# The end of an RNN-and-attention kernel rewritten as one written list: who subtracts the maxima, where transposes go, when outputs are projected

## The chip, the cores and the metric

The kernel runs on one core of a Trainium2 chip, in fp32 throughout. The metric is the time of one execution in microseconds (us) on the device; the figure of a kernel is the median of several executions. A profile is one further execution, recorded by the hardware profiler.

## The reference, cut to what matters

The input `x` has shape (2, 2048, 256). Layer one is a recurrent layer on the normalized input with a residual; layer two is an attention layer whose values and outputs are mixtures of five experts, again on the normalized input with a residual. Only the second layer and its end bear on this case:

```python
e, d, dh = Wv.shape                       # 5, 256, 64; 8 heads
wv = _topk_mask(gl_v, SEL) * sigmoid(gl_v)
xv = einsum('btd,edk->btek', x, Wv)
v = einsum('bthe,btek->bhtk', wv, xv)
scores = einsum('bhid,bhjd->bhij', q * scale, k)
probs = softmax(scores, axis=-1)
attn = einsum('bhij,bhjd->bihd', probs, v)
mask_o = _topk_mask(gl_o, SEL)
out = einsum('bthe,bthk,ekd->btd', mask_o, attn, Wo)
```

So each (batch, head) has 2048 x 2048 scores, a softmax over the keys, a product with the values; each head's result is then spread over the five experts that its mask selects (320 numbers per position), summed over the heads, and multiplied by `Wo` as one 320 x 256 product. The result is added to the residual and written out.

## The kernel before, in words

The recurrent layer takes the first 120 us or so and is left alone by the change. After it, `x1d` in DRAM holds the residual stream.

**Units, steps and tiles.** The attention is cut into 64 units (`units`): 16 (batch, head) pairs by four blocks of 512 queries. A unit has eight tiles of scores; a tile is two blocks of 128 keys by 512 queries, 128 x 1024 numbers, and its index is `t` (unit 63 has tiles 504 to 511, unit 62 has 496 to 503). One step `T` of the loop at the end of the function makes two tiles, so a unit takes four steps (`U_T`), and there are 256 steps (`NT`).

**What happens to a tile.** `scores` (L634) multiplies on TensorE into a PSUM tile of two banks (pool `ps_s`, two buffers, four banks). `stage` (L645) copies it to SBUF on ScalarE; `largest` (L655 to L661) keeps the running maximum on VectorE. When a unit's eight tiles are in, `turn_max` and `reduce_max` (L668, L673) turn the maxima with four TensorE transposes and reduce them on VectorE, and `spread_max` (L683, L686) transposes the result back so that all partitions hold each query's maximum, once in PSUM (`pt`) and, copied by ScalarE, once in SBUF (`top`). `subtract` (L693) takes the maximum off a staged tile: tiles 0 and 1 of a unit on VectorE from `pt`, the others on GpSimd from `top`; in the last unit tiles 0, 1, 2, 4 and 6 are VectorE's. `exponential` (L696) is ScalarE's. `products` (L706) accumulates P.V on TensorE into `o`. `fold` (L718) adds a tile's odd partner into it by a DMA that accumulates, issued from GpSimd, so that `sums` (L727), which accumulates the softmax's denominators on TensorE, takes half as many tiles; in the last unit nothing is folded and all eight tiles are summed. A tile's second half of life runs `LAG` = 6 steps behind its scores.

**The end of a unit.** `take` (L742, L743) and `take_sums` (L749, L750) bring `o` and the sums `d` to SBUF; `weigh` (L759 to L768) transposes them and works out reciprocal times mask; `close` (L772) makes the 320 wide product `pro` on VectorE; `gather` (L814, L817) adds `pro` into `yd` in DRAM, or, for the last head, into `y` in SBUF that `fetch_y` (L793) has brought, on GpSimd. `close_last` (L772, L804) does the same for the very last unit on VectorE, 128 positions at a time.

**The outputs.** 16 blocks of 128 positions per batch. `turn_out` transposes a block of `y` (`py`, L829, three transposes), copies it to one of two `yT` tiles on ScalarE (L833, L836), and loads the residual `z` from `x1d` (L838, on SP's queue). `project_out` multiplies by `Wo` (`pz`, L846, twelve matmuls that the profile counts as 24), adds `pz` into `z` on VectorE (L854), and stores `z` (L855, SP). `z` has two buffers (pool `ap`, `bufs=2`), so the load of block c+2 waits until the store of block c has landed. The small PSUM tiles `pm`, `pt`, `po`, `py`, `pz` all come from `misc`, two banks in turn.

**What sets the order.** Each engine executes its queue in order. The order is written by hand: three tables (`before`, `first_behind`, `behind`) say which helper is called in which step, and the loop over `T` runs over `NT + LAG + 1` steps, so that the last seven steps do only what lags behind. The outputs of the last two units (blocks 8 to 15 of batch 1) and the `close_last` between them are queued in one piece in the last step. There is no planner; within this part the compiler keeps the traced order on each engine, and it places tiles in the banks that their pools come to hold.

Of the kernel before, what the change touches and what calls it, by code (L numbers as in the profile page):

```python
# [8 lines left out]
F32 = mybir.dt.float32  # L9
# [5 lines left out]
P = 128  # L15
# [5 lines left out]
def rnn_then_switchhead_kernel(  # L21
# [15 lines left out]
    nc = tc.nc  # L37
# [82 lines left out]
    def misc(shape, nm):  # L120
        return ps_m.tile(shape, F32, tag="m", name=nm)
# [95 lines left out]
    def choose(pool, b, c0, n, half, nm, logits):  # L217
# [16 lines left out]
        for d in range(1, E):  # L234
            a = pool.tile([P, n, H, E - d], F32, tag=f"later{d}", bufs=1 + (d > 1), name=f"lt{nm}_{d}")
            nc.vector.tensor_tensor(a, g0[:, :, :, d:E], g[:, :, :, 0 : E - d], ALU.is_gt)
            later.append(a)
# [324 lines left out]
    four = ctx.enter_context(tc.tile_pool(name="four", bufs=1))  # L562
    ps_s = ctx.enter_context(tc.tile_pool(name="ps_s", bufs=2, space=PSUM))
    ps_o = ctx.enter_context(tc.tile_pool(name="ps_o", bufs=1, space=PSUM))
    units = [(i, n) for i in range(len(heads)) for n in range(NQ)]
    NT = len(units) * U_T
# [81 lines left out]
    def largest(t, ss):  # L648
# [13 lines left out]
        m_of.pop(u)  # L662

    def turn_max(u):
        pm = misc([P, QS, P], f"pm{u}")
        mm = mm_of.pop(u)
        for s in range(QS):
            nc.tensor.transpose(pm[:, s, :], mm[:, s * P : (s + 1) * P], ident)  # L668
        mx_of[u] = (pm, ap.tile([P, QS], F32, tag="mq", name=f"mq{u}"))
# [5 lines left out]
    def spread_max(u):  # L675
        _, mq = mx_of.pop(u)
        if u == len(units) - 1:
            pt = ps_s.tile([P, 2, QB], F32, tag="s", name=f"pt{u}")[:, 0, :]
            pt = pt.rearrange("p (s q) -> p s q", q=P)
        else:  # L680
            pt = misc([P, QS, P], f"pt{u}")
        for s in range(QS):
            nc.tensor.transpose(pt[:, s, :], mq[:, s : s + 1].to_broadcast([P, P]), ident)  # L683
        pt = pt.rearrange("p s q -> p (s q)")
        top_of[u] = (pt, ap.tile([P, QB], F32, tag="top", name=f"top{u}"))
        nc.scalar.copy(top_of[u][1], pt)  # L686

    def subtract(t):
        u, c = t // HC, t % HC
        p = ring[t]  # L690
        last = u == len(units) - 1 and c % 2 == 0
        eng, top = (nc.vector, top_of[u][0]) if c < 2 or last else (nc.gpsimd, top_of[u][1])
        eng.tensor_tensor(p, p, top.unsqueeze(1).to_broadcast([P, 2, QB]), ALU.subtract)  # L693
# [100 lines left out]

    def close_last(u):

        i, n = units[u]
        b, _ = heads[i]
        po, mr = weigh(u)
        y = y_of[b, n]  # L800
        pr = four.tile([P, QS, E, DH], F32, tag="pro", bufs=1, name=f"pro{u}")
        for s in range(QS):
            masked(pr[:, s : s + 1], po, mr, s, 1)
            nc.vector.tensor_tensor(y[:, s], y[:, s], pr[:, s], ALU.add)  # L804

    def gather(u):
# [18 lines left out]
    def turn_out(b, c):  # L825
        yf = y_of[b, c // QS][:, c % QS].rearrange("p e k -> p (e k)")
        py = misc([P, len(o_chunks), P], f"py{b}_{c}")
        for k, (r0, m) in enumerate(o_chunks):
            nc.tensor.transpose(py[0:m, k, :], yf[:, r0 : r0 + m], ident)  # L829
        yT = yT_all[yT_of["n"] % 2]  # L830
        yT_of["n"] += 1
        full = sum(m == P for _, m in o_chunks)
        nc.scalar.copy(yT[:, 0:full, :], py[:, 0:full, :])  # L833
        for k, (r0, m) in enumerate(o_chunks):
            if m < P:
                nc.scalar.copy(yT[0:m, k, :], py[0:m, k, :])  # L836
        z = ap.tile([P, D], F32, tag="z", name=f"z{b}_{c}")
        nc.sync.dma_start(out=z, in_=x1d[c, :, b, :])  # L838
        yT_of[b, c] = (yT, z)
# [137 lines left out]
    for u, (i, n) in enumerate(units):  # L977
        b, h = heads[i]
        T1 = (u + 1) * U_T
        at(first_behind, T1, spread_max, u)  # L980
        outs = [(b, n * QS + s) for s in range(QS)]
        if u == len(units) - 1:

            outs = [(b, c) for c in range(n * QS - QS, n * QS + QS)]
            todo = [(turn_out, *outs[0])]
            for k, o in enumerate(outs):
                todo += [(turn_out, *x) for x in outs[k + 1 : k + 2]] + [(project_out, *o)]
            at(behind, T1 + LAG - 1, fetch_y, u)
            for x in todo[:3] + [(take_sums, u), (close_last, u)] + todo[3:]:
                at(behind, T1 + LAG, *x)  # L990
            continue
        at(behind, T1 + LAG + 1, take_sums, u)
        at(behind, T1 + LAG + 2, close, u)
        at(behind, T1 + LAG + 3, gather, u)
        if h == H - 1:
            at(behind, T1 + LAG, fetch_y, u)
            if u < len(units) - 2:
                T = T1 + LAG + 4
                for o, t, p in zip(outs, (0, 1, 3, 3), (1, 2, 3, 4)):
                    at(before if o[1] % QS == 2 else behind, T + t, turn_out, *o)  # L1000
                    at(behind if o[1] % QS == 2 else before, T + p, project_out, *o)

    with tc.manual_schedule():
        for T in range(NT + LAG + 1):
            new = (2 * T, 2 * T + 1) if T < NT else ()
            sub = [t for t in (2 * (T - LAG + 1), 2 * (T - LAG + 1) + 1) if 0 <= t < 2 * NT]
# [9 lines left out]
            ss = [scores(t) for t in new]  # L1016
            if new:
                stage(new[0], ss[0])
            if T % U_T == 0:
                if new:  # L1020
                    stage(new[1], ss[1])
                if 0 < T <= NT:
                    turn_max(T // U_T - 1)
                    reduce_max(T // U_T - 1)
                if new:
                    largest(new[1], ss[1])
            elif new:
                largest(new[1], ss[1])
                stage(new[1], ss[1])
            if fresh:  # L1030
                subtract(sub[0])
            if T % U_T and new:
                largest(new[0], ss[0])
# [4 lines left out]
            k = T - LAG  # L1038
            if 0 < k < NT - U_T + 1:
                fold(2 * (k - 1))  # L1040
# [4 lines left out]
            for t in old:  # L1045
                products(t)
            if 3 <= k and k % 2 and k - 3 < NT - U_T:
                t = 2 * (k - 3)
                sums(t, t + 2, t % HC == 0, t % HC != 0)
            if NT - 2 <= k < NT:  # L1050

                t0 = 2 * (NT - U_T)
                for t in range(t0, t0 + 4, 2) if k == NT - 2 else ():
                    sums(t, t + 1, t == t0, False)
                sums(2 * k, 2 * k + 1, False, k == NT - 1)
            if sub:
                exponential(sub[0])
            for f in first_behind.pop(T, []) + behind.pop(T, []):
                f()
        assert not before and not behind and not first_behind  # L1060


# [44 lines left out]
```

## Time and profile before

| | |
|---|---|
| median of 3 runs | 1616.0 us (1615.15 to 1617.99) |
| the profiled execution's own time | 1618.95 us |
| its span, first to last instruction | 1617.2 us |
| mean granted TensorE clock | 0.992 |
| busy: TensorE, VectorE, ScalarE, GpSimd | 95%, 80%, 77%, 79% of the span |
| end of the last scores | about 1546.4 us |
| first and last add of an output of batch 1 (L854) | 1549.7 and 1613.8 us |

The page of the profile gives busy time by engine, then the span in 40 slices; views can be asked for any stretch of it. In a view by windows each row is a stretch with its length, then busy time and number of instructions of each engine, then the granted clock and the DMA's share. In a list of groups, a row has the line, engine, operation, output<-inputs, shapes and count, then busy time and mean ns of one, then the idle time just ahead. The profile counts an fp32 matmul as two or more instructions.

### The profile page before, as it was taken

Reading aid. Unit: us, or ns where it says so; the run is one execution under the profiler, and the core shown is the slowest. Engines: PE = TensorE matmul, PEld = TensorE weight load, DVE = VectorE, ACT = ScalarE, POOL = GpSimd, SP = SyncE. Lnnn points to the kernel's source line nnn. Section 1 sums busy time; section 2 is a strip of 40 time slices with the busy share of each in tenths; the row PEclk is TensorE's granted clock in tenths of the full one; section 3 lists DMA queues with packets and bytes.
Section 4 is the critical chain, followed back from the end, with each engine's and each line's share of the span. In section 5 each row is a group of like instructions: output and inputs, shape, how many; then the busy total and the mean of one; then the engine's idle time right before and its main releaser. Section 6 shows DMA issues by size and latency. Waiting matters only on the chain.

```text
span 1617.2 us, 29233 instructions
## 1 busy us (share of the span) xinstructions
PE 1540.3 (95%) x11442; PEld 593.7 (37%) x11442; DVE 1297.6 (80%) x1808; ACT 1251.0 (77%) x1617; POOL 1285.5 (79%) x856
## 2 busy tenths in 40 slices
PE   6989899999999999999999999999999999999996
PEld 5984233333333333333334333333333333333233
DVE  7472889998988888888987769898889888888762
ACT  4664688888878888888887778888888888888861
POOL 3053699888888988999997868898889898889870
PEclk9998999999999999999999999999999999999998
DMA  5021368788888888787886767788888888888752
GB/s 162 1 106 31 105 152 192 163 187 179 173 167 173 173 172 174 157 178 164 171 188 156 168 143 187 154 177 171 174 165 176 176 169 170 169 170 170 165 130 83
DMA packets 86623, 252.26 MB, mean 156 GB/s; under 512 B 11920, under 2 KB 31184, under 8 KB 86480
## 3 DMA queue, kind: packets, MB, share of 16 engines
q0 software_dynamic: 43200, 163.60, 54.0%
q1 hardware_dynamic: 41648, 86.13, 17.5%
q8 instruction: 91, 1.49, 0.4%
q10 hardware_dynamic: 1632, 0.61, 0.1%
q14 instruction: 52, 0.43, 0.1%
HBM read 59.46 MB, written 50.33 MB: 68 GB/s over the span
## 4 chain that ended last, share of the span: by engine, by line
PE 67%; DVE 12%; DMA 6%; ACT 3%; issue 2%; POOL 2%; SPq 0%; DVEq 0%; ACTq 0%; POOLq 0%
PE s L634 23%; PE o L706 20%; PE d L727 6%; DVE m L655 5%; DMA p<-p 4%; PE pk L140 4%; PE pq L159 3%; PE pz L846 2%; ACT p L645 2%; PE pt L683 2%; DVE pro L772 2%; PE pm L668 1%; POOL p L693 1%; PE po L759 1%; DVE p L693 1%
## 5 line engine op out<-in xcount | busy, mean ns | idle before, releaser
L693 POOL TENSOR_TENSOR p<-p,top 128x1024 f32<-128x1024 f32 x381 | 1057.2, 3027 | 11.8 <-ACT top L686 11.7
L645 ACT COPY p<-s 128x1024 f32<-128x1024 f32 x512 | 511.0, 1011 | 152.8 <-DVE m L655 66.9
L696 ACT ACTIVATE p<-p 128x1024 f32<-128x1024 f32 x512 | 538.0, 1062 | 49.5 <-DVE p L693 37.1
L634 PE MATMUL s<-qs,k 64*128 64x512 f32 x1024 | 511.8, 617 | 6.4 <-ACT p L645 6.3
L634 PE MATMUL s<-q,k 64*128 64x512 f32 x1024 | 511.8, 617 | 4.0 <-ACT p L645 3.2
L706 PE MATMUL o<-p,v 128*32 128x512 f32 x4096 | 491.5, 597 | 10.2 <-DVE os L743 7.7
L655 DVE TENSOR_TENSOR m<-s,m 128x1024 f32<-128x1024 f32 x320 | 390.9, 1222 | 96.4 <-PE s L634 87.7
L718 POOL DMA_DIRECT2D p<-p x252 | 341.4, 1355 | 60.0 <-PE o L706 21.5
L706 PEld LDWEIGHTS o<-p,v 128*32 128x32 f32 x4096 | 113.5, 109 | 297.8 <-issue 156.4
L634 PEld LDWEIGHTS s<-qs,k 64*128 64x128 f32 x1024 | 169.1, 186 | 144.1 <-ACT p L645 47.9
L634 PEld LDWEIGHTS s<-q,k 64*128 64x128 f32 x1024 | 169.1, 185 | 138.7 <-issue 52.4
L693 DVE TENSOR_TENSOR p<-p,pt 128x1024 f32<-128x1024 f32 x131 | 158.5, 1210 | 0.1
L727 PE MATMUL d<-p,ones 128*32 128x512 f32 x1040 | 153.1, 593 | 5.1 <-DMA p<-p 5.0
L655 DVE TENSOR_TENSOR m<-s,p 128x1024 f32<-128x1024 f32 x64 | 78.4, 1225 | 57.5 <-ACT p L645 57.1
L814 POOL DMA_DIRECT2D yd<-pro x48 | 45.2, 942 | 92.0 <-DVE pro L772 89.8
L772 DVE TENSOR_TENSOR pro<-po,mr 128x1280 f32<-128x1280 f32 (+1 forms) x67 | 95.9, 1431 | 2.7
L619 DVE TENSOR_TENSOR xq<-xq,wp 128x1280 f32<-128x1280 f32 x60 | 89.2, 1487 | 2.3 <-DVE wp L617 0.2
L625 DVE TENSOR_REDUCE v<-xq 128x256 f32<-128x1280 f32 x60 | 88.6, 1477 | 0.0
L727 PEld LDWEIGHTS d<-p,ones 128*32 128x32 f32 x1040 | 37.5, 110 | 97.2 <-issue 76.8
L159 PE MATMUL pq<-xn2T,wq 128*32 128x512 f32 x512 | 63.3, 612 | 6.3 <-DVE rtd L427 6.3
L140 PE MATMUL pk<-xn2T,wk 128*32 128x512 f32 x512 | 62.2, 604 | 0.0
L673 DVE TENSOR_REDUCE mq<-pm 128x4 f32<-128x512 f32 x64 | 44.3, 692 | 18.3 <-PE pm L668 16.9
(172 smaller groups left out, 1478.4 us busy)
## 6 DMA issues: line engine op xcount, KB each, us to landing
p<-p POOLq DMA_DIRECT2D x252, 512.0 KB, 6.2
xq<-xvd SPq DMA_DIRECT2D x60, 640.0 KB, 5.2
yd<-pro POOLq DMA_DIRECT2D x48, 640.0 KB, 7.3
qs<-q SPq DMA_DIRECT2D x64, 128.0 KB, 2.8
yd<-pro SPq DMA_DIRECT2D x8, 640.0 KB, 4.1
y<-yd SPq DMA_DIRECT2D x8, 640.0 KB, 6.0
x<-in_x SPq DMA_DIRECT2D x16, 256.0 KB, 6.0
x1d<-x SPq DMA_DIRECT2D x16, 256.0 KB, 2.0
```

The lines of the kernel that those rows point to most:

```text
L140: nc.tensor.matmul(pk[at_col : at_col + 32], lhsT=wk[:, kc, h * DH + g : h * DH + g + 32], rhs=xc[:, kc, c0 // 2 : (c0 + HC) // 2, o, :], ...
L159: nc.tensor.matmul(pq[at_col : at_col + 32, :], lhsT=wq[:, kc, h * DH + g : h * DH + g + 32], rhs=xn2T[:, kc, b, n * QB : (n + 1) * QB], s ...
L619: nc.vector.tensor_tensor(xq, xq, wp.unsqueeze(2).to_broadcast([P, 4, DH, E]), ALU.mult)
L634: nc.tensor.matmul(ss[:, o, :], lhsT=k_of[i][half, c, :], rhs=q_of[i, n][o][half, :], start=True, stop=True,)
L645: nc.scalar.copy(p, ss)
L655: nc.vector.tensor_tensor(m, ss, ring[t - 1] if c == 1 else m, ALU.max)
L693: eng.tensor_tensor(p, p, top.unsqueeze(1).to_broadcast([P, 2, QB]), ALU.subtract)
L696: nc.scalar.activation(ring[t], ring[t], AF.Exp)
L706: nc.tensor.matmul(o_of[u][at_col : at_col + 32, :], lhsT=v_of[i][:, 2 * c + o, g : g + 32], rhs=ring[t][:, o, :], start=c == 0, stop=c == ...
L718: nc.gpsimd.dma_start(out=ring[t], in_=ring.pop(t + 1), accum_op=ALU.add)
L727: nc.tensor.matmul(den_of[u][32 * g : 32 * (g + 1), :], lhsT=ones32, rhs=ring[(t, t1)[g // 2]][:, g % 2, :], start=first, stop=last, tile_ ...
L772: nc.vector.tensor_tensor(dst, po[:, s : s + n, 0:DH].unsqueeze(2).to_broadcast([P, n, E, DH]), mr[:, s : s + n].unsqueeze(3).to_broadcast ...
```

## The change

All that stands behind the last scores (the last seven steps of the loop) becomes a written list, `drain()`. The loop now runs over 256 steps and does nothing special at its end; helpers that the tables would have put behind it are left out of the tables and stand in the list. In it:

- the four banks of `ps_s` are closed after the loop and opened as pool `ps_z` with four one-bank buffers; `pt` and `py` come from there (`other`), so `misc` keeps `pm`, `pz` and `po`;
- unit 62's maxima are spread a second time into PSUM, and VectorE subtracts tile 502; of the last unit VectorE subtracts tiles 504 to 510 (seven, it was five), GpSimd only 511;
- the last unit's tiles 504 to 507 are folded by two DMAs, and `sums` of that unit are three calls instead of four;
- outputs stand between the products: in the list's order blocks 1 to 7 are projected before the last unit's sums, then 8 and 9, and blocks 10 to 15 in the new `close_last`, which takes each 128 positions of the last unit as they are ready; `take_sums`, `close` and `gather` of unit 61 come earlier or later as the list has them;
- `z` gets three buffers; to make room, the tile `later4` of the gates (`choose`) has one buffer instead of two;
- `ps_o` is opened ahead of `ps_s`, so the two pools hold other banks than before from the start of the attention on.

```diff
-            a = pool.tile([P, n, H, E - d], F32, tag=f"later{d}", bufs=1 + (d > 1), ...)
+            a = pool.tile([P, n, H, E - d], F32, tag=f"later{d}", bufs=1 + (1 < d < 4), ...)
-    ps_s = ctx.enter_context(tc.tile_pool(name="ps_s", bufs=2, space=PSUM))
     ps_o = ctx.enter_context(tc.tile_pool(name="ps_o", bufs=1, space=PSUM))
+    scores_only = ctx.enter_context(ExitStack())
+    ps_s = scores_only.enter_context(tc.tile_pool(name="ps_s", bufs=2, space=PSUM))
+    spare = {}
+    def other(nm):
+        return spare["pool"].tile([P, QB], F32, tag="z", name=nm)
     def spread_max(u):
-        if u == len(units) - 1:
-            pt = ps_s.tile([P, 2, QB], F32, tag="s", name=f"pt{u}")[:, 0, :]
+        if spare:
+            pt = other(f"pt{u}_").rearrange("p (s q) -> p s q", q=P)
...
+        if u in top_of:
+            top_of[u] = (pt, top_of[u][1])
+            return
-    def subtract(t):
+    def subtract(t, on_vector=False):
-        last = u == len(units) - 1 and c % 2 == 0
-        eng, top = (nc.vector, top_of[u][0]) if c < 2 or last else (nc.gpsimd, top_of[u][1])
+        on_vector |= c < 2
+        eng, top = (nc.vector, top_of[u][0]) if on_vector else (nc.gpsimd, top_of[u][1])
-    def close_last(u):
+    def close_last(u, outs):
...
-        for s in range(QS):
+        def ready(s):
             masked(pr[:, s : s + 1], po, mr, s, 1)
             nc.vector.tensor_tensor(y[:, s], y[:, s], pr[:, s], ALU.add)
+        ready(0)
+        project_out(*outs[0])
+        ready(1)
+        project_out(*outs[1])
+        for s in range(QS):
+            turn_out(*outs[2 + s])
+            if s + 2 < QS:
+                ready(s + 2)
+            if s:
+                project_out(*outs[1 + s])
+        project_out(*outs[-1])
-        py = misc([P, len(o_chunks), P], f"py{b}_{c}")
+        py = other(f"py{b}_{c}")[:, : len(o_chunks) * P] if spare else misc(...)
-        z = ap.tile([P, D], F32, tag="z", name=f"z{b}_{c}")
+        z = ap.tile([P, D], F32, tag="z", bufs=3, name=f"z{b}_{c}")
+    def drain():
+        w, v, u = len(units) - 3, len(units) - 2, len(units) - 1
+        tv, tu = HC * v, HC * u
+        turned, projected = 2, 1
...
+        spread_max(v); turn_max(u); subtract(tv + 6, True); subtract(tv + 7)
+        reduce_max(u); take_sums(w); exponential(tv + 5); project(); spread_max(u)
+        products(tv + 4); products(tv + 5); fold(tv + 2); fold(tv + 4)
+        exponential(tv + 6); exponential(tv + 7); subtract(tu, True)
+        close(w); gather(w); turn(); fetch_y(v)
+        exponential(tu); subtract(tu + 1, True); exponential(tu + 1)
+        subtract(tu + 7); subtract(tu + 2, True)
+        products(tv + 6); products(tv + 7); fold(tv + 6)
+        turn(); project(); take(v); sums(tv, tv + 2, True, False); project()
+        exponential(tu + 2); subtract(tu + 3, True); exponential(tu + 3); subtract(tu + 4, True)
+        products(tu); products(tu + 1); turn(); fold(tu); subtract(tu + 5, True)
+        exponential(tu + 4); turn(); project()
+        products(tu + 2); products(tu + 3); fold(tu + 2)
+        sums(tv + 4, tv + 6, False, True); take_sums(v)
+        exponential(tu + 5); subtract(tu + 6, True); turn(); project()
+        exponential(tu + 6); products(tu + 4); products(tu + 5); exponential(tu + 7)
+        turn(); fetch_y(u); project(); close(v); gather(v)
+        products(tu + 6); products(tu + 7); take(u); project()
+        sums(tu, tu + 2, True, False); sums(tu + 4, tu + 5, False, False)
+        sums(tu + 6, tu + 7, False, True); take_sums(u)
+        turn(); turn(); project(); turn(); project(); turn()
+        close_last(u, outs[-QS - 2 :])
-        for T in range(NT + LAG + 1):
+        for T in range(NT):
...
+        scores_only.close()
+        spare["pool"] = ctx.enter_context(tc.tile_pool(name="ps_z", bufs=4, space=PSUM))
+        drain()
```

In the list above several calls stand on one line where the code has one to a line; `turn()` and `project()` call `turn_out` and `project_out` for the next block.

## The prediction, made before the changed kernel was run

> **What bounds the kernel now.** I read first the page's busy times, then the span by windows behind the last scores, then the chain of work that ended last, then the waits of that stretch, by engine.
>
> Windows from the end of the last scores (columns: window, length, busy us and instructions of PE, PEld, DVE, ACT, POOL, then clock and DMA):
>
> ```profile
> 1546.40:1551.00 4.60, 4.60 (x54) 2.05 (x55) 3.54 (x5) 3.23 (x5) 4.60 (x4) 1.00 0.46 89
> 1551.00:1582.00 31.00, 27.84 (x310) 11.47 (x312) 14.75 (x22) 16.51 (x27) 18.43 (x10) 1.00 0.53 128
> 1582.00:1617.20 35.20, 21.55 (x263) 10.46 (x255) 9.73 (x23) 5.85 (x20) 1.71 (x1) 0.88 0.29 91
> ```
>
> TensorE is 95% busy over the whole span, but from 1582 on only 21.6 us of 35.2, and no other engine is near full. The tail is 70.8 us long, and its last third is bound by something else. The chain shows by what (start us, us, what):
>
> ```profile
> 1604.15 2.31 DMA out<-z
> 1606.46 0.02 issue
> 1606.48 0.32 SPq L838
> ...
> 1606.85 2.09 DMA out<-z
> 1608.93 0.02 issue
> ...
> 1609.00 0.32 SPq L838
> ...
> 1609.37 2.25 DMA out<-z
> 1611.62 0.02 issue
> 1611.63 2.06 DMA z<-x1d
> ```
>
> A store of an output lands, and only then SP issues the next load of `z` and, behind it, the next store: one output per 2.6 us (1606.48 to 1609.00 to 1611.63), where TensorE needs 1.8 for one. The waits from 1546.4 on (total us, times, longest):
>
> ```profile
> DVE z L854 <- DMA z<-x1d: 18.1, 8, 3.8
> DVE z L854 <- PE pz L846: 6.4, 4, 2.2
> PE pz L846 <- ACT yT L836: 2.9, 5, 0.7
> PE po L759 <- DVE os L750: 2.8, 1, 2.8
> PE pz L846 <- DVE z L854: 2.2, 2, 1.3
> ```
>
> VectorE stands 18.1 us at the residuals, and what is behind it in its queue stands too: the sums of the last unit (L750) had been ready at 1588.2 and were added at 1591.28, behind the add of 1590.82, and TensorE waited 2.8 us for them. That idling has a second price, seen in a finer answer by windows:
>
> ```profile
> 1592.00:1595.00 3.00, 2.22 (x15) 1.57 (x19) 1.56 (x6) 0.53 (x2) 0.00 (x0) 0.50 0.30 87
> 1595.00:1598.50 3.50, 3.50 (x31) 1.37 (x27) 2.97 (x7) 0.24 (x1) 0.00 (x0) 0.50 0.00 0
> ```
>
> The clock fell to 0.50: one projection took 2.79 us there, 1.50 elsewhere.
>
> **What the Trainium skill says.** "TensorE: Matmul & The Clock Gate", Part 1: the clock is halved after about one idle window of 3.4 us, and comes back after about one busy one. The trace agrees: between 1588.0 and 1592.0 TensorE was busy for 1.33 us, then came 0.50. "DMA: Bandwidth & Descriptors", Anatomy of one DMA: about 2.0 us of a transfer are fixed (said of GpSimd's path; these are SP's). Here a 128 KB load or store takes 2.06 to 2.31 us from issue when little else moves, so no engine's speed shortens that round trip, and only more buffers hide it. "SBUF — State Buffer", Who interferes with whom: a VectorE operation on two tensors locks GpSimd's reads out if both inputs are in SBUF. A subtraction from `pt` reads PSUM and SBUF, so moving subtractions to VectorE should slow neither. No row here isolates that; GpSimd's own subtractions spread from 2.36 to 3.66 us.
>
> **The change part by part.** I walk down the engines' queues as the compiled order of the two kernels has them (that order is known without a run), each instruction starting when its engine is free and its inputs are there. Durations are from the rows behind 1546: on TensorE one projection 1.30 when another follows (48 rows took 2.80, 24 took 1.50), a turned block 0.49, a tile's products 0.86 (16 rows 1.72), a call of sums 0.86 (24 rows 2.58), four transposes 0.60; VectorE subtraction 1.14 (1.21 alone), add 0.43, `pro` 1.49; ScalarE exponential 1.06, `yT` copies 0.27 each and 0.1 until the first is done; GpSimd subtraction 2.45 (2.84 at worst in the mean), `y` add 2.93; fold 0.9 of issue and 5.0 to land; `z` load 0.38 + 2.1, store 0.34 + 1.9, `y` 4.4; 0.05 from one engine to another.
>
> *The same walk on the kernel before*, from 1550.9 (the last thing common to both queues on TensorE is a turned block that ends there), puts the last add (L854) at 1613.3; the trace has 1613.8. The clock's fall is not in the walk, so it flatters nothing by more than that half us. On this I rely.
>
> *TensorE's account, before.* From 1550.9 to 1611.2: 15 projections 19.5, 14 turned blocks 6.9, 12 tiles of products 10.3, six sums 5.2, five times four transposes 3.0, together 44.9 of 60.3 us. The other 15.4: waits 10.8 (2.9 + 2.8 + 2.2 above, and 1.6, 0.7, 0.6 from the same list), half of the 5.7 us busy at half clock 2.8, the rest ends of matmuls.
>
> *After: work.* One sums call less (-0.86; the folds of 504 and 506 cost GpSimd two DMA issues and no TensorE), one spreading of unit 62 more (+0.60): 44.6.
>
> *After: VectorE and GpSimd.* VectorE has eight subtractions instead of five, 3 x 1.21 = 3.6 us more on an engine busy 28 of 70.8; GpSimd loses three, 8.5 us, so the last unit's exponentials need not wait for its three in a row. GpSimd's later work (adds of `pro61` and `pro62`, three folds) then stands behind only one subtraction. In the walk the fold of 502 lands 1.1 us late for its sums; that is the one stall GpSimd still makes. The cover of the eight subtractions is TensorE's products and projections; without it they would cost 3.6.
>
> *After: queues.* SP issues the same 2 `y` loads and `z` transfers. The load of `y1_2` is moved ahead of the load of `z` 3 and waits for the third turned block to free its buffer (1559.2 in the walk); `z` 3 behind it lands at 1562 and is wanted at 1562.9, hidden by under one us. The `y` of the last unit is fetched at about 1575, lands near 1579, wanted at 1589.
>
> *After: idle of TensorE in the walk.* Before the last sums 0.1 + 0.1 + 0.2 (the take of `o` ahead of the last unit's products) + 0.4 (copies of `yT` for block 4) + 1.1 = 1.9; its 29.7 us of work then end at 1582.5, with seven blocks projected since 1550.9, where before only the five blocks 1 to 5 were, by 1581.5. Behind that, eight turned blocks, eight projections and one `po`, 14.9 us, with 0.3 + 1.45 idle: in `close_last`, projection 11 wants the `misc` bank of `po`, which VectorE has read only after its first four small operations and block 10's add. End 1599.2, against 1611.2. The last `z` load waits for the store of block 12 and lands late by 1.5, so the last add starts at 1600.8.
>
> *The sum.* 1613.3 - 1600.8 = 12.5 us between the two walks. Of it the third buffer alone is worth 4.4 (the walk before with three buffers), and the new list with two buffers 8.9 (1604.4); together they give a little less than their sum. The end of the span stays 3.4 us behind the last add (1617.2 - 1613.8).
>
> *Other edits.* `later4` with one buffer: its next writer could wait for GpSimd's reader. In the trace that reader is done at 674.7, 721.5 and 765.6, the writers come at 699.7, 744.3, 788.6; in the first batch 154.0 against 156.5. Nothing. *The banks*: with `ps_o` first, the first tile of scores no longer shares banks with the transposes of the step before, and its two halves come into TensorE's queue among them. Before, the first scores waited 0.64 us for ScalarE's last copy (136.5 to 137.1); both halves of a tile run beside each other, 0.96 us, and apart they take 0.96 each. So 0.96 - 0.64 = +0.3, or up to +1.0 if nothing is saved, down to -0.6 if the split is free; I take +0.2.
>
> Against the profiled execution: 1618.95 - 12.5 + 0.2 = 1606.6, span 1604.9. The median of the runs lies 2.95 below the profiled time, so 1616.0 - 12.3 = 1603.7 us.
>
> Varying one price at a time in both walks: GpSimd subtraction 3.2, difference 12.7; fold landing in 6.5, 12.5; VectorE 1.22, 12.5; `z` load 2.9, 14.9; store 2.4, 14.6; all at once 16.2. So the bounds are uneven, with more gain than loss: 1600 to 1605 for this case.
>
> **Rivals.** *A: the outputs keep the pace of the round trip.* For: the load of `z` stands in SP's queue behind stores which wait for VectorE, so a third buffer may be free and not used. Against: with three buffers a load waits for the store of three blocks before, 3 x 1.8 = 5.4 us of TensorE's work earlier, and the round trip is 2.3 + 2.4. Price: the walk with two buffers, +3.6: 1607.3. *B: the clock falls again*, where TensorE idles before projection 11 or at the fold. For: 1.33 busy in 4 us was enough before; against: the longest idle in the walk is 1.5. Price 2.8: 1606.5. *C: only the buffer counts* and the order gives nothing, as VectorE with eight subtractions becomes the tail's bound: 1616.0 - 4.4 = 1611.6; against it, VectorE is busy 28 + 3.6 of some 58. *D: slower.* The moved banks shift the phase in which scores, ScalarE's copies and VectorE's maxima follow each other; in the loop TensorE already waits for ScalarE's copies (L645) 9.5 us at scores. One more wait of this kind per unit, 64 times, eats the 12.3 gained at 0.19 us each; above 0.24 each the kernel is slower by over 0.2% (1619.2). Against: from step 1 on the engines' queues are the same.
>
> **How the numbers follow.** Forecast 0.76, A 0.08, B 0.08, C 0.04, D 0.04, half of D within 0.2% and half slower. 0.2%, 3.2 us, is about what a measurement of this kernel can tell from no change. The range 1600.0 to 1607.6 takes in the forecast's bounds, A and B. Faster 0.96, same 0.02, slower 0.02.
>
> **What would show it.** Right: last scores within 0.5 us of 1546.4; waits of L854 for `z` well under 18 us; seven blocks projected by the last sums, near 1582.5; clock 1.00 to the end; last add near 1601. Wrong: a clock of 0.50 in the tail (B), stores and loads alternating at 2.6 us at the end (A), VectorE without idle there (C), last scores later by 10 us (D).

## The result, and the profile after

| | before | after |
|---|---|---|
| median | 1616.34 us (1615.15 to 1617.99, 4 runs) | 1605.22 us (1604.87 to 1606.15, 4 runs) |
| ratio of after to before | | 0.9935 (95%: 0.9921 to 0.9949) |
| the profiled execution: own time, span | 1618.95, 1617.2 us | 1606.15, 1604.4 us |
| end of the last scores | 1546.39 us | 1543.13 us |
| from there to the end of the span (the tail) | 70.8 us | 61.3 us |
| mean granted clock | 0.992 | 0.997 |

The forecast was 1603.7 us for the median and 1604.9 for the span; measured are 1605.2 and 1604.4. The two lower rows show that this agreement has two halves that the forecast didn't have: the last scores end 3.26 us earlier, where nothing was expected, and the tail is 9.5 us shorter, where 12.5 were. The agreement of the span is therefore luck in part: an early end of the scores covers a loss behind them. Nearly all that follows asks where these two halves come from.

The span by windows behind the last scores (length, busy us and instructions of PE, PEld, DVE, ACT, POOL, then clock and DMA), cut at the end of the last sums, and two shorter stretches:

```profile
1543.10:1551.00 7.90, 7.80 (x93) 3.85 (x95) 6.32 (x9) 5.59 (x9) 7.79 (x5) 1.00 0.47 102
1551.00:1582.90 31.90, 28.77 (x307) 11.28 (x300) 16.71 (x25) 14.67 (x27) 11.64 (x7) 0.95 0.76 182
1582.90:1604.40 21.50, 15.48 (x220) 8.60 (x219) 8.09 (x20) 4.59 (x17) 0.00 (x0) 0.98 0.31 94
1562.00:1565.20 3.20, 0.07 (x2) 0.01 (x1) 2.96 (x4) 1.37 (x4) 0.42 (x1) 1.00 1.08 202
1566.00:1569.40 3.40, 3.40 (x28) 1.01 (x20) 0.05 (x1) 0.67 (x3) 0.04 (x1) 0.52 0.91 192
```

Behind the last sums (third row) TensorE is busy for 15.5 us of 21.5, 72%; from 1582 on it was 21.6 of 35.2 before, 61%. But in the middle there are two small stretches that tell of a loss: 3.2 us in which TensorE did next to nothing (0.07 us of work), and right behind them 3.4 us at half clock.

The waits from 1546.4 on (total us, times, longest):

```profile
DVE z L876 <- PE pz L868: 8.4, 5, 2.7
...
DVE z L876 <- DMA z<-x1d: 6.4, 3, 3.0
ACT p L705 <- DVE p L702: 6.3, 3, 4.4
```

VectorE's residual add is L876 now (L854 before). Its wait for `z` fell from 18.1 us to 6.4, and it waits longer for TensorE's projections than for the loads: that is the sign of the round trip being hidden in the main. The end of the chain:

```profile
1596.88 1.75 DMA out<-z
...
1598.69 2.10 DMA z<-x1d
...
1600.99 0.42 DVE z L876
```

Only one round trip of store and load is left in the chain of the tail's last stretch, that of the last block. Before, the chain went from round trip to round trip.

**The loss in the middle**, from the lists of instructions in order of time (start us, us, engine, line, operation; in brackets the idle time ahead and what ended it). SP's queue, VectorE's, ScalarE's and TensorE's; the third line is from the chain of work and gives the load's time from issue to landing:

```profile
1555.85 0.32 SPq L802 DMA_DIRECT2D y<-yd  x1
1556.27 0.97 SPq L860 DMA_DIRECT2D z<-x1d  x1
1556.27 5.90 DMA z<-x1d
1562.24 0.42 DVE L876 TENSOR_TENSOR z<-pz,z 128x256 f32<-128x256 f32 x1 [3.05 <-DMA z<-x1d]
1562.58 3.47 DVE L702 TENSOR_TENSOR p<-p,pt__14118 128x1024 f32<-128x1024 f32 x3
1563.83 1.06 ACT L705 ACTIVATE p<-p 128x1024 f32<-128x1024 f32 x1 [4.40 <-DVE p L702]
1564.79 0.35 ACT L855 COPY yT<-py 128x256 f32<-128x256 f32 x1
1565.20 1.91 PE L868 MATMUL pz<-wo,yT 128*32 128x256 f32 x24 [3.13 <-ACT yT L855]
1566.86 3.25 PE L715 MATMUL o<-p,v 128*32 128x512 f32 x16
```

Read it from the top. SP issues the load of `y1_2` (640 KB, the `y` of batch 1 that unit 62 needs) and at 1556.27 that of `z` 3, the residual of block 3, which takes 5.90 us to land. VectorE stands 3.05 us at the add of block 3. The three subtractions of the last unit behind it in its queue stand with it; ScalarE waits 4.40 us for the first of them, tile 507; the copies of `yT` for block 4 are behind that exponential in ScalarE's queue; and TensorE, four links away from the load, waits 3.13 us for the copies. Then the clock falls for 3.4 us: a pair of tiles' products takes 3.25 us instead of 1.92, and the projection ahead of it 1.91 instead of 1.50. One load of 128 KB that comes late by 3 us costs TensorE 3.1 us, and then some 1.7 more.

**The head.** The order of TensorE's work at the start of the attention, before and then after: projection of queries, the first group of the gates' logits (`pgd`), half of the first keys (`pk`), the second group of logits. Start us and us:

```profile
125.70 3.70 PE L489 MATMUL pgd<-wsd,xn2T 128*128 128x80 f32 x16
129.33 2.67 PE L140 MATMUL pk<-xn2T,wk 128*32 128x512 f32 x16
131.93 2.01 PE L489 MATMUL pgd<-wsd,xn2T 128*128 128x80 f32 x16
...
139.04 1.92 PE L140 MATMUL pk<-xn2T,wk 128*32 128x512 f32 x16
```

```profile
126.98 1.93 PE L140 MATMUL pk<-xn2T,wk 128*32 128x512 f32 x16
128.84 2.01 PE L489 MATMUL pgd<-wsd,xn2T 128*128 128x80 f32 x16
...
131.22 1.12 PE L635 MATMUL s<-q,k 64*128 64x512 f32 x2
...
133.29 1.12 PE L635 MATMUL s<-qs,k 64*128 64x512 f32 x2
...
135.99 1.92 PE L140 MATMUL pk<-xn2T,wk 128*32 128x512 f32 x16
```

The same keys take 2.67 us in one profile and 1.93 in the other: before's profile had the half clock for 13.65 us around here (117.2 to 130.9), after's for 6.8 (118.9 to 125.7). That is 1.83 us of the 3.26 (from the start of the queries' projection, 122.13 and 120.87, to the second logits: 9.80 and 7.97). Another 1.26 were there already when that projection started, from the recurrent layer, which the change doesn't touch. The banks' own place is the stretch from the second logits to the second half of the keys: 7.11 us before (131.93 to 139.04), 7.15 after (128.84 to 135.99). From there to the last scores it is 1407.35 us before and 1407.14 after: the loop is the same. 1.26 + 1.83 - 0.04 + 0.21 = 3.26.

### The profile page after: what moved, and what is told of

The parts are those of the page before. It is cut to its first block, busy times and chain, and to the rows that moved or that the text cites. A ratio compares the mean times of both kernels' runs of the same rounds, so it can differ in the third digit from the quotient of the medians.

```text
span 1604.4 us, 29221 instructions
## 1 busy us (share of the span) xinstructions
PE 1536.7 (96%) x11438; PEld 592.6 (37%) x11438; DVE 1300.1 (81%) x1811; ACT 1250.1 (78%) x1617; POOL 1278.1 (80%) x855
## 4 chain that ended last, share of the span: by engine, by line
PE 67%; DVE 13%; DMA 5%; ACT 3%; issue 2%; POOL 2%; SPq 0%; DVEq 0%; ACTq 0%; POOLq 0%
PE s L635 23%; PE o L715 20%; PE d L736 6%; DVE m L656 5%; DMA p<-p 4%; PE pk L140 4%; PE pq L159 3%; PE pz L868 2%; ACT p L646 2%; DVE pro L781 2%; PE pt L689 2%; PE pm L675 1%; DVE p L702 1%; POOL p L702 1%; PE po L768 1%
## 5 line engine op out<-in xcount | busy, mean ns | idle before, releaser
L702 POOL TENSOR_TENSOR p<-p,top 128x1024 f32<-128x1024 f32 x378 | 1046.6, 3007 | 11.5 <-ACT top L695 11.4
L705 ACT ACTIVATE p<-p 128x1024 f32<-128x1024 f32 x512 | 538.1, 1062 | 51.0 <-DVE p L702 39.7
L727 POOL DMA_DIRECT2D p<-p x254 | 337.3, 1329 | 69.5 <-PE o L715 21.6
L702 DVE TENSOR_TENSOR p<-p,pt 128x1024 f32<-128x1024 f32 x126 | 152.3, 1209 | 0.0
L680 DVE TENSOR_REDUCE mq<-pm 128x4 f32<-128x512 f32 x64 | 44.3, 692 | 18.3 <-PE pm L675 16.9
```

The source lines that it names most:

```text
L705: nc.scalar.activation(ring[t], ring[t], AF.Exp)
L727: nc.gpsimd.dma_start(out=ring[t], in_=ring.pop(t + 1), accum_op=ALU.add)
```

## The experiments

Theory: the late landing of `z` 3 is what the tail lost. Three readings of it are tried: the load is late because it stands behind 640 KB of `y1_2` on SP's queue (Q); it is late because the DMA engines are full of folds (F); and, whichever of these holds, the wait hurts only by what VectorE has queued behind the add (V). Rivals: the parts were worth less than the walk said even without it (the buffer, the list, VectorE's subtractions, the scores' banks); the earlier last scores come from the pools' new banks and not from chance. All ratios are to the kernel before, measured beside each group of runs (its medians there went from 1615.3 to 1616.9 us, so ratios compare better than medians), with 95% intervals. The tail is that of one profiled execution, from the end of its last scores to the end of its span. Two profiles with the same tail code, before and e4, have tails 1.0 us apart, with the half clock in them for 6.8 and 3.4 us; so a difference of 1 us between two tails shows nothing by itself.

| kernel | median us (runs) | ratio | tail us |
|---|---|---|---|
| before | 1616.34 (4) | 1 | 70.8 |
| after | 1605.22 (4) | 0.9935 (0.9921 to 0.9949) | 61.3 |
| e3: before, three `z` | 1612.15 (22) | 0.9977 (0.9968 to 0.9986) | 67.4 |
| e2: after, two `z` | 1609.05 (6) | 0.9951 (0.9932 to 0.9970) | 64.2 |
| e4: before, pools' order | 1615.93 (14) | 1.0001 (0.9991 to 1.0011) | 69.8 |
| e5: after, subtractions as before | 1605.40 (6) | 0.9925 (0.9904 to 0.9945) | 60.2 |
| e7: after, `py` from `misc` | 1608.57 (6) | 0.9945 (0.9925 to 0.9966) | 61.9 |
| e1: `z` 3 loaded ahead of `y1_2` | 1601.81 (6) | 0.9914 (0.9898 to 0.9930) | 57.8 |
| e6: block 3's add behind the subtractions | 1602.69 (6) | 0.9918 (0.9898 to 0.9937) | 58.6 |
| e9: e1 with four `z` | 1601.18 (6) | 0.9909 (0.9886 to 0.9931) | 57.3 |
| e8: e1 and e6 | 1602.66 (4) | 0.9906 (0.9891 to 0.9920) | 59.2 |
| e11: e1 and e6, four `z` | 1604.13 (5) | 0.9920 (0.9907 to 0.9933) | 57.2 |
| e10: a fold later | 1607.83 (6) | 0.9947 (0.9934 to 0.9960) | 63.0 |

**e3, the buffer alone.** The kernel before, with the third `z` and one `later4`:

```diff
-            ... tag=f"later{d}", bufs=1 + (d > 1), ...
+            ... tag=f"later{d}", bufs=1 + (1 < d < 4), ...
-        z = ap.tile([P, D], F32, tag="z", name=f"z{b}_{c}")
+        z = ap.tile([P, D], F32, tag="z", bufs=3, name=f"z{b}_{c}")
```

> The kernel before with three buffers of z instead of two (and one buffer of later4, for room); nothing else. The walk gives -4.4 us: about 1612 us, waits of the add for z from 18 down to under 9 us, last outputs each 1.9 instead of 2.6 us apart. Rival (SP's queue order keeps the loads at the round trip's pace, a third buffer is not used): 1616. Rival (the buffer was all of the change): 1605.

Its waits at the residuals from the last scores on:

```profile
DVE z L854 <- PE pz L846: 11.7, 7, 2.9
DVE z L854 <- DMA z<-x1d: 5.1, 2, 2.8
```

From 18.1 us of waiting for `z` to 5.1 by one buffer and with nothing moved; VectorE now waits for TensorE. Yet the tail is only 3.4 us shorter (forecast 4.4) and the median 3.2: with the old order TensorE still waits 2.5 us for the last unit's sums (2.8 before), and the half clock still follows, for 6.8 us as before. That the buffer alone counts (rival C) is out, and so is that a third buffer lies idle (rival A).

**e2, the list alone.** After, with two `z`:

```diff
-        z = ap.tile([P, D], F32, tag="z", bufs=3, name=f"z{b}_{c}")
+        z = ap.tile([P, D], F32, tag="z", bufs=2, name=f"z{b}_{c}")
```

> The changed kernel with two buffers of z instead of three: the new order without the new buffer. My walk gives +3.6 us over the changed kernel: about 1608.9 us, waits of the add for z from 6.4 to over 12 us. Together with the run of the buffer alone (3.2 us in the median) it says whether list and buffer add up. Rival (the list is worth nothing, the buffer all): 1615. Rival (the buffer is idle under the new order): 1605.

```profile
DVE z L876 <- DMA z<-x1d: 12.2, 5, 3.4
```

Tail 6.6 us shorter than before (walk: 8.9), median 7.2. The list with two buffers waits twice as long for `z` as with three, and has the stall before block 4 too (TensorE idle for 3.47 us). 3.4 + 6.6 = 10.0 against 9.5 for both together: the parts add up to about the whole (a little more, as the walk had it, but by no more than tails differ), and all three are short of the walk by a quarter.

**e4, the pools' order alone.** Before, with `ps_o` opened first:

```diff
-    ps_s = ctx.enter_context(tc.tile_pool(name="ps_s", bufs=2, space=PSUM))
     ps_o = ctx.enter_context(tc.tile_pool(name="ps_o", bufs=1, space=PSUM))
+    ps_s = ctx.enter_context(tc.tile_pool(name="ps_s", bufs=2, space=PSUM))
```

and `later4` with one buffer as well.

> The kernel before with the two PSUM pools opened in the changed kernel's order, and later4 with one buffer; nothing in the tail. In the changed kernel's profile the last scores ended 3.3 us earlier than before. Theory H (that came from TensorE's clock, which in the profile of before was at half for 6.8 us longer around the start of the attention, and is chance): within 1.5 us of the kernel before in the median, and from the second group of logits to the second half of the first keys about 7.1 us as before. Rival (the moved banks let the attention start 3 us earlier): about 1613.

The same two places of TensorE's list as in the head above:

```profile
130.07 2.01 PE L489 MATMUL pgd<-wsd,xn2T 128*128 128x80 f32 x16
...
137.22 1.92 PE L140 MATMUL pk<-xn2T,wk 128*32 128x512 f32 x16
```

7.15 us between them, as in after, against 7.11 before: the banks cost 0.04 us. The time is the same within 0.1%. Its last scores end at 1543.65 and those of e3, which has before's banks, at 1542.1; so the 3.3 us at the head are no work of the banks. They go with executions, not with kernels: in e7's profile, which has after's banks, the last scores end at 1546.8, as late as before. Rival D is out, and so is a gain from the pools' order.

**e5, VectorE's new subtractions given back.** After, with tiles 502, 507 and 509 on GpSimd:

```diff
-        subtract(tv + 6, True)
+        subtract(tv + 6)
...
-        subtract(tu + 3, True)
+        subtract(tu + 3)
...
-        subtract(tu + 5, True)
+        subtract(tu + 5)
```

> The changed kernel with the subtractions of tiles 502, 507 and 509 given back to GpSimd. My walk: +0.3 us, 1605.5, because GpSimd has room and the exponentials of 507 and 509 come at about the same time. If VectorE's taking them is what the change lives on: 1608 or more, with ScalarE's exponentials waiting for GpSimd. If VectorE's load is what holds its adds of outputs: faster, 1603.

```profile
DVE z L876 <- DMA z<-x1d: 8.7, 4, 4.8
...
ACT p L705 <- POOL p L702: 4.8, 2, 4.5
```

Giving the three subtractions back changes nothing that can be measured: median 1605.4, tail 1.1 us shorter. But this doesn't show that they are worth nothing. ScalarE waits 4.5 us for GpSimd's subtraction of tile 507 where it waited 4.40 for VectorE's, TensorE idles 2.73 us before block 4 instead of 3.13, and half clock follows for 3.4 us as in after: GpSimd's own queue makes the same stall that the late `z` makes in VectorE's. What VectorE's subtractions are worth when `z` 3 is in time, no run shows.

**e7, the transposes back in `misc`.**

```diff
-        py = other(f"py{b}_{c}")[:, : len(o_chunks) * P] if spare else misc([P, len(o_chunks) * P], f"py{b}_{c}")
+        py = misc([P, len(o_chunks) * P], f"py{b}_{c}")
```

> The changed kernel with the turned blocks of y back in misc's two banks, as before; the spread maxima stay in the scores' banks. My walk: +1.1 us, 1606.3, from TensorE waiting for VectorE's adds before it may turn the next block. If the banks are the heart of the change: +5 us, 1610. If they are not used: 1605.2.

```profile
PE pz L868 <- DVE z L876: 2.1, 2, 1.3
PE py L851 <- DVE z L876: 1.5, 2, 1.0
```

These are the waits that the two extra banks take away: TensorE waiting for VectorE to read the bank that the next transpose or projection wants (2.2 us of this kind before, 0.8 in after). The tail is 0.6 us longer (the walk: 1.1), but that is not the whole price: the clock did not fall in this tail, because a turned block that waits 0.98 us now stands in the stall before block 4 and leaves 2.08 us of idle in one piece. Without half clock, e7 is spared the 1.7 us that after lost so; my estimate from the two traces is that the banks are worth some 2 us of the tail. The median is 3.4 us above after's, five of the six runs took over 1608 us, which none of after's or e5's did, and yet the ratios (0.9945 and 0.9935) have overlapping intervals. The waits above say that the banks give something; whether it is the walk's 1.1 us or three times as much stays open.

**e1, `z` 3 ahead of `y1_2` on SP's queue (Q).**

```diff
         turn()
-        fetch_y(v)
         exponential(tu)
...
         turn()
+        fetch_y(v)
         project()
```

> The changed kernel with one line moved: the fetch of unit 62's y (640 KB) stands behind the residual load of block 3 in SP's queue instead of ahead of it. Theory Q (the tail lost 3 us of its forecast because that 128 KB load landed 5.9 us after its issue, behind the 640 KB; VectorE stood 3.0 us at its add with three subtractions behind it, TensorE 3.1 us behind those, and the clock then fell to half for 3.4 us): the load lands within 3.5 us, the wait at block 3 is under 0.5 us, the clock is 1.00 in the tail, tail from last scores to the end 58.0 to 58.8 us instead of 61.3, time 2 to 3.5 us under the changed kernel's 1605.2. Rival R (the DMA engines are full there with the accumulating folds, and the order on SP does not matter): block 3's load still lands after more than 5 us, tail 61 us, time 1605.

VectorE at block 3's add, TensorE at block 4's projection and the products behind it:

```profile
1558.84 0.42 DVE L876 TENSOR_TENSOR z<-pz,z 128x256 f32<-128x256 f32 x1 [1.15 <-DMA z<-x1d]
...
1561.80 1.50 PE L868 MATMUL pz<-wo,yT 128*32 128x256 f32 x24 [1.23 <-ACT yT L855]
1563.12 1.90 PE L715 MATMUL o<-p,v 128*32 128x512 f32 x16
```

TensorE's idle time falls from 3.13 to 1.23, and with it the half clock goes: 1.90 us for what took 3.25. The tail is 57.8 us, 3.5 shorter than after's (1.9 us less idle and the 1.7 of the clock account for it), and within 0.5 of the forecast's 58.3 (70.8 - 12.5). But the load itself did not get quick, which Q had expected (within 3.5 us). The chain of this kernel gives it

```profile
1551.21 7.55 DMA z<-x1d
```

7.55 us instead of 5.90. It helps because SP issues it 9.6 us behind the last scores (1541.63) and not 13.1 (1556.27 - 1543.13). So it lands 17.1 us behind them and not 19.0, and VectorE's wait falls by just these 1.9 us. Q is right that the place in the queue costs, and wrong on why: what helped is the time at which SP comes to the load, while without the 640 KB ahead of it the load took longer.

**e6, block 3's projection and add behind the subtractions (V).** Late as it is, the load then has nothing of ScalarE's behind it:

```diff
         sums(tv, tv + 2, True, False)
-        project()
         exponential(tu + 2)
         subtract(tu + 3, True)
         exponential(tu + 3)
         subtract(tu + 4, True)
+        project()
```

> The changed kernel with the projection of block 3 placed behind the subtractions of tiles 507 and 508, so that VectorE's add of block 3 no longer stands ahead of them; TensorE's and SP's orders are as in the changed kernel. Theory Q: the late load is then waited for behind the two subtractions, the exponential of 507 is not held, TensorE does not idle 3.1 us before block 4's projection, the clock stays at 1.00; tail 58 to 59 us, time about 1602 to 1603. Rival R2 (TensorE idled before block 4 because block 4's own copies were late, whatever VectorE did): tail stays 61 us.

```profile
1561.97 1.50 PE L868 MATMUL pz<-wo,yT 128*32 128x256 f32 x24 [0.19 <-ACT yT L855]
...
1563.29 1.90 PE L715 MATMUL o<-p,v 128*32 128x512 f32 x16
```

TensorE's wait is 0.19 us, no half clock follows, the tail is 58.6 us. It comes to this although VectorE still waits longest for a `z`, now one block later:

```profile
1569.91 0.43 DVE L876 TENSOR_TENSOR z<-pz,z 128x256 f32<-128x256 f32 x1 [6.46 <-DMA z<-x1d]
```

6.46 us of VectorE's waiting here cost TensorE 0.28 us at its next projection and 0.69 at the transposes behind it, while 3.05 us in after cost it 3.13 and the clock. What counts is what is queued behind the wait.

**e10, the folds that fill the DMA engines (F).** The fold of tile 500 later, so that only one 512 KB accumulating DMA (that of tile 498) is queued near z 3's load:

```diff
         fold(tv + 2)
-        fold(tv + 4)
...
         products(tv + 7)
+        fold(tv + 4)
         fold(tv + 6)
```

> The changed kernel with one DMA moved: the fold of tile 500 (512 KB, adding) is issued right ahead of the fold of 502 instead of some 8 us before. In the changed kernel the load of block 3's z took 5.9 us from its issue, with that fold and the 640 KB of y in flight; with y behind it, it took 7.5. Theory F (the folds keep the DMA engines busy, and this is what makes the load late): the load lands within 4 us, the wait at block 3 falls from 3.0 to under 1 us, the clock stays 1.00 there, tail about 58.5 instead of 61.3 us, time 1602 to 1603, unless the sums of 500 and 502 wait for the later fold, which shows at L736. Theory Y (y's 640 KB ahead of it do): the load still takes over 5 us, time 1605.

```profile
1555.58 0.38 SPq L860 DMA_DIRECT2D z<-x1d  x1
...
1559.61 0.42 DVE L876 TENSOR_TENSOR z<-pz,z 128x256 f32<-128x256 f32 x1 [1.10 <-DMA z<-x1d]
...
1569.91 1.05 PE L736 MATMUL d<-p,ones 128*32 128x512 f32 x4 [3.06 <-DMA p<-p]
...
1571.37 2.78 PE L868 MATMUL pz<-wo,yT 128*32 128x256 f32 x24
```

With the same `y1_2` ahead of it the load lands within 3.9 us of its issue (1555.58 to about 1559.5) instead of 5.9, and VectorE waits 1.10 and not 3.05: F is right on the landing. The traces show it at work: in after, GpSimd's queue, which carries the folds, fills the DMA engines from 1555.0 to 1557.4 (110% of their time by the profile's count) while SP's queue gets 2.6%; in e10, from the load's issue to its landing, only SP's queue moves data. F is not all of it: 3.9 us is still 1.8 above the 2.1 of a load near the end, and no run separates how much of that the 640 KB make. The time is not better (tail 63.0), since the sums now wait 3.06 us for the late folds, and again half clock follows (2.78 us for a projection of 1.5). The transfers are too many for this stretch; moving one moves the wait.

**e9, e8, e11: is more to be had?** e9 is e1 with four `z` (and one buffer for every `later` tile), e8 is e1 and e6 in one, e11 both with four `z`.

> The run with block 3's load ahead of unit 62's y (1601.8), with four buffers of z instead of three and, for room, one buffer for each of the gates' later tiles. My walk gives -1.2 us: 1600.6, the adds' waits for z (10.0 us in that run) halved. If what is left is the DMA engines being full (the load of block 3 took 7.5 us there though issued 5 us earlier), waits at block 3 and 4 stay and the time is 1601.8.

> The changed kernel with both repairs: block 3's load ahead of unit 62's y, and block 3's projection behind the subtractions of 507 and 508. In the first alone TensorE still waits 1.2 us before block 4's projection, in the second alone VectorE still waits 6.5 us at block 4's add. Expected: 1600.5 us, 1 us under each alone; if each already removed the whole stall, 1602.

> Both repairs and four buffers of z (later tiles single): expected 1600, no more than 1 us under the two repairs, since the run with four buffers and one repair was 0.6 us under that without. If the waits of the adds for z in the end (2.6 us at most) come from SP's queue order and not from buffers: same as the two repairs.

The waits for `z` in e9, and VectorE's longest wait in e8:

```profile
DVE z L876 <- DMA z<-x1d: 11.6, 6, 3.1
```

```profile
1569.49 0.42 DVE L876 TENSOR_TENSOR z<-pz,z 128x256 f32<-128x256 f32 x1 [7.48 <-issue]
```

The fourth buffer doesn't shorten the waits (11.6 us; 10.0 in e1), so buffers aren't what holds the loads any more; the tail is 0.5 us shorter and the time the same within its interval. In e8 the two cures together gave 1602.66 where 1600.5 was expected. A likely reason is that they stand in each other's way: with the add later, block 3's store is later, and the load of `z` 4 stands behind that store on SP (issued from 1561.30 on, 19.2 us behind the last scores; 18.1 in e1). The view names no releaser for VectorE's wait ("issue"), so this is read from the order and not shown. e11 was expected at 1600 and came at 1604.13, although its profiled execution (1601.76) has a tail of 57.2; that miss stays open. All five kernels with block 3 cured have ratios from 0.9906 to 0.9920, and after, e5, e7 and e10 from 0.9925 to 0.9947. Single intervals of the two groups overlap, so it is the traces of e1 and e6, more than their times, that show the cause; the fastest median, e9's 1601.18, is 4.0 us below after's and can't be told from e1's 1601.81.

## Why the prediction was right, and where it was not

*The bound.* Right: behind the last scores the store and load of `z` set the pace, and the three waits that stood for it (18.1 us for `z`, a 2.8 us wait of TensorE for the last unit's sums, the clock's fall) are gone or smaller (half clock for 3.4 us of the tail's middle, 6.8 before). e3 and e2 show that buffer and list each take a part.

*The sum.* 12.5 us were forecast for the tail and 9.5 came. In time from the last scores: the last sums were to end 36.1 us behind them (1582.5 - 1546.4) and ended 39.7 behind (1582.86 - 1543.13), 3.6 us later; 0.5 of that the forecast had in hand, since its walk of the kernel before ended 0.5 us ahead of the trace. From there to the last add it took 18.1 us, with 18.3 forecast. So the stretch behind the last sums was right to 0.2 us, and the whole loss lies before it. Whoever only checks "last sums near 1582.5, last add near 1601" finds both marks met (1582.86 and 1600.99) and misses it: the marks were absolute and the scores ended 3.3 us early.

*The step that failed* is "`z` 3 behind it lands at 1562 and is wanted at 1562.9, hidden by under one us". It landed at 1562.16, but with scores 3.26 earlier it was wanted at 1559.2; seen from the last scores it was 3.4 us late. The term mis-sized is the load's 0.38 + 2.1 = 2.5 us, taken from loads with little else under way: it took 5.90 (7.55 in e1). Of these 3.4 us too many, 2.0 are the fold of tile 500 in the DMA engines (e10: 3.9 without it there); the rest came with `y1_2` in flight and isn't separated. The profile before had the sign: between 1552 and 1566, with three folds issued, its two loads of `z` took

```profile
z<-x1d SPq DMA_DIRECT2D x2, 128.0 KB, 4.4
```

4.4 us in the median from issue to landing. Of the Trainium skill's page "DMA: Bandwidth & Descriptors", Anatomy of one DMA, I used the fixed 2.0 us as nearly the whole time of a small transfer; here that held at the end of the tail (2.10) and not in its middle (5.90). The variation in the prediction, "`z` load 2.9" at most, was too narrow, and it was applied to both walks, so that it showed more gain, not less. With 5.90 for this one load the walk gives 1.55 us less gain; the half clock behind it costs 1.7 (3.25 - 1.92 in the products, 1.91 - 1.50 in the projection). Together that is 3.3, about the 3.0 that were missing; the 1.55 is the walk's figure, which no run measures.

*Rival B* (the clock falls again) came true in the tail, at another place than named: not at projection 11, where the idle was 0.81 us for 1.45 forecast, but behind the 3.13 us before block 4. The idle that cost the clock was 3.13 us here and 3.06 in e10; after 1.23 in e1 it didn't. What the prediction cites from the Trainium skill, "TensorE: Matmul & The Clock Gate", Part 1, a halving after about one idle window of 3.4 us, gives the size; but here shorter idle times were enough (2.5 us in e3 and e4, and 1.7 at one place each of e7 and e8), so that a longest idle of 1.5 us in a walk is a thinner margin than the prediction took it for.

*A third term made up for it.* The head was forecast at +0.2 and came at -3.3: banks +0.04 (the half that I called "free" is nearly so: two parts of a tile stand in 1.12 us of busy time each, and the whole stretch is 0.04 longer), the rest differences between executions, in when the recurrent layer ends and how long the half clock lasts behind it. The profiled execution of before was its slowest, 2.6 us above the median, that of after 0.9 above its own; so of the 12.8 us between the two profiles 1.7 are not in the medians, which differ by 11.1. How the remaining 1.6 beside the tail's 9.5 divide between the head and the tail of executions without a profile stays open.

*VectorE's subtractions.* Their cost was not hidden throughout: three of them stood behind the late `z`. Taking them back to GpSimd (e5) made neither gain nor loss, but there GpSimd's subtraction of 507 stood on the path instead, so their own gain stays open. The fold of 502, expected 1.1 us late for its sums, showed no wait in after, where all in front of it was 3 us late.

*What of the range.* 1605.2 lies inside 1600.0 to 1607.6; the kernels with block 3 cured have tails of 57.2 to 59.2 us, so the forecast's tail of 58.3 was that of a kernel whose order in SP's or VectorE's queue is right in one more place.

## What to carry to other kernels

Price a transfer by what is in flight beside it at that time, not by its size alone, and vary that price only in the kernel where the traffic is new. For each wait that is "hidden by under one us", list what stands behind it on its engine and on the engines fed by those: here one late load reached TensorE through VectorE, a subtraction, an exponential and a copy, and changing either the load's place (e1) or the add's place (e6) ended the most of it. Give marks relative to the stage's own start, so that luck at the head can't cover a loss behind it.

## What the runs showed of the hardware that was not expected

- A 128 KB load on SP's queue took 2.1 us at the end of the tail, and 3.9, 5.9 and 7.55 us in its middle (e10, after, e1), with a mean DMA share of 0.57, 0.68, 0.73 and 1.03 from issue to landing. While a fold's packets filled the DMA engines in after (1555.0 to 1557.4), SP's queue got 2.6% of their time.
- TensorE's half clock followed every idle time of 2.5 us or more in the attention (2.52 in e3, 2.54 in e4, 2.73 in e5, 2.78 before, 3.06, 3.13 and 3.47 in e10, after and e2). Of shorter ones it followed 1.69 us in e7 (at 454.8) and 1.75 in e8 (at 1500.6), but not 2.08 in e7's tail. Where the span's end doesn't cut it off, it lasted 3.4 us or a multiple of that: 6.8, 10.2 (e5 and e6, start of the attention) or 13.65.
- Executions of like kernels differ by some 5 us at the end of the last scores (1541.6 in e1, 1546.4 in before's profile, 1546.8 in e7), part of it by how long the half clock lasts around the start of the attention.
